# When the reciprocals of three blocks' denominators are taken in the keys stage of a decoder layer

## The chip, the cores and the metric

The kernel runs on one core of a Trainium2 chip. The metric is the device time of one execution in microseconds (us), the median of three runs; lower is better. Besides the times there is one execution recorded by the hardware profiler. A core has five engines that run side by side and wait for each other through semaphores: PE (matrix products; PEld is its weight loading), DVE (vector operations), ACT (activations and casts), POOL (a second, slower vector engine) and SP, which here only issues transfers (DMA). Each of them works through its own queue in order.

## The reference, cut to what matters

```python
x = x + attn(layernorm(x))             # linear attention, 16 heads, 128 features per head
x = x + xattn(layernorm(x), ctx)       # cross-attention to 154 context rows
x = x + ffn(layernorm(x))              # 8 experts, the 6 best per token, and a shared part

# attn, for each of 2 batches of 2048 tokens of width 512:
q_proj, k_proj = elu1(q @ proj), elu1(k @ proj)
kv    = einsum('bhnf,bhnd->bhfd', k_proj, v)
attn  = einsum('bhnf,bhfd->bhnd', q_proj, kv)          # numerators
z     = 1.0 / (einsum('bhnf,bhf->bhn', q_proj, k_proj.sum(axis=2)) + 1e-08)
out   = (attn * z[..., None]).reshape(b, n, d) @ w_out + b_out
```

Everything is in float32. The reciprocal `z` is what the change is about: one number for each token and head.

## The kernel before, in words

The 4096 tokens are 8 blocks of 512 (`nblk`), 4 to each batch (`bpb`). A product of full accuracy is written as three matrix multiplications of rounded parts (`product`, line 144).

The **keys stage** (lines 1323 to 1350) runs over the keys of all 8 blocks, 16 steps to a block, one for each chunk `c` of four heads and each tile `t` of 128 tokens. A step makes the key features (`key_features`: a matrix product `pp`, two ACT activations at lines 371 and 372, one DVE operation at line 373 and an addition on POOL at line 414) and now and then adds them to the sums (`key_values`, `pkv`). While the second batch's keys are worked, the same steps also make the query features of the first batch (`query_step`, `pqp`, from step 66 on), because that batch's sums are finished. When a chunk of queries is complete, `sums_step` takes its numerators (`pn`, copied by DVE at line 509 and stored by SP at line 510) and its denominators (`pd`). After the fourth chunk of a block, `reciprocals` is called.

Between the steps `dense` fills in other products: a list of generators that give one matrix multiplication at a time. Here these are the queries, keys and values of the next blocks (`pq`, `pk`, `pv`), and in the last block the keys and values of the context for the cross-attention (`xpk`, `xpv`). `dense` also is the clock of the program: `dense.after(n, do)` runs `do` when `n` more multiplications of the list have been recorded.

`reciprocals(b, pd)` (line 529) does in this order:

- DVE adds the small constant and copies `pd` out (`den`, line 532); SP writes it to memory in four pieces (`dd`, line 535).
- 10 products later (`turned`, line 541) SP loads it back as a tile `z` of 128 rows, so that the reciprocal is short.
- 26 products after the denominators (`stored`, lines 544 and 545) DVE takes the reciprocal of `z`, held at its place in the program's order, and SP stores the result (`zd`). The last block has 24.

The readers of `zd` are `load_reciprocals` (line 558, tiles `zr`, loaded by SP at the end of the keys stage and in the queries stage that follows) and then `attended` (line 570 on POOL, 571 on ACT, 118 on DVE). The attention's output products (`po_a`) follow, with the weight `wout`, which is loaded (`xswout`) and split into two parts (`split_weight`, lines 138 and 118: `wout_hi` on ACT, `wout_lo` on DVE and POOL) in the last block of the keys stage.

Three things tie the queues to each other. The banks of the accumulators are few: `pp` and `pqp` share four (`sc`), `pq`, `pn`, `pd`, `pkv`, `xpk` and the like share four others. The half tiles that hold `e_k`, `e_q`, `num`, `den` and `kf` share nine buffers (`kp`), so a new one may have to wait until SP has stored an old one. And each of SP's transfers waits for the one eight places before it.

The order in which the instructions stand in the queues is settled when the program is built: a scheduler with a modelled time line orders them within what the dependences allow (`schedule_with_timeline_sim=True`), except where `keep_in_program_order` holds one.

Of the kernel before, what the change touches and what calls it, by code (L numbers as in the profile page):

```python
# [37 lines left out]
def decoder_layer(  # L38
# [28 lines left out]
    nblk = tokens // TB  # L67
    bpb = nblk // batches
# [32 lines left out]
    def half(name, dtype=F32):  # L101
        return work.tile([P, 512], dtype, tag="kp", name=name, bufs=9)
# [115 lines left out]
    dense = Dense()  # L218
# [121 lines left out]
    for t in range(NT):  # L340
# [5 lines left out]
        b = nc.vector.tensor_tensor(lo, pt, hi.bitcast(F32), ALU.subtract)  # L346
# [167 lines left out]
    def denominators(b, c):  # L514
        if c == 0:
            pds[b] = bank(f"pd{b}")
        for h in range(4):
            columns.matmul(
                pds[b][h * HD : (h + 1) * HD, :],
                lhsT=kszs[b // bpb][:, c, h, :],  # L520
                rhs=qps.pop((b, c, h)),
                start=c == 0,
                stop=c == NC - 1,
                skip_group_check=True,
            )
        if c == NC - 1:
            reciprocals(b, pds.pop(b))

    def reciprocals(b, pd):

        den = half(f"den{b}")
        nc.vector.tensor_scalar(den, pd, Z_EPS, None, ALU.add)
        dd = dram.tile([4, NC, TB], F32, name=f"dd{b}")
        for h in range(4):
            nc.sync.dma_start(out=dd[h], in_=den[h * HD : h * HD + NC, :])
        z = small.tile([P, H * TB // P], F32, tag="z", name=f"z{b}", bufs=1)
        flat = "h c n -> (h c n)"
        zd = dram.tile([4, NC, TB], F32, name=f"zd{b}")

        def turned():  # L540
            nc.sync.dma_start(out=z, in_=dd.rearrange(flat).rearrange("(p n) -> p n", p=P))

        def stored():
            tc.keep_in_program_order(nc.vector.reciprocal(z, z))
            nc.sync.dma_start(out=zd.rearrange(flat).rearrange("(p n) -> p n", p=P), in_=z)

        dense.after(10, turned)
        dense.after(26 if b < nblk - 1 else 24, stored)
        zds[b] = zd

    def load_numerators(b):
# [771 lines left out]
    for n in range(nblk * per):  # L1323
        b, c, t = n // per, n // NT % NC, n % NT
# [38 lines left out]
    for n in range(len(steps) + 1):  # L1363
        if n < len(steps):
            b, c = steps[n]
# [41 lines left out]
    for n in range(len(steps) + LAG + 1):  # L1407
        if n < len(steps):
            b, c, t = steps[n]
# [46 lines left out]
        if n > LAG:  # L1456
            b, c, t = steps[n - LAG - 1]
# [187 lines left out]
```

## Time and profile before

| what | value |
|---|---|
| median of three runs | 2317.7 us (2314.31 to 2324.51) |
| the profiled execution | 2318.24 us, span 2316.5 us, mean PE clock 0.989 |
| PE, PEld busy | 2226.9 us (96%), 1729.3 us (75%) |
| DVE, ACT, POOL busy | 1682.5 us (73%), 1103.5 us (48%), 1231.5 us (53%) |
| transfers | 498.24 MB, mean 215 GB/s |
| reciprocals (line 544) | 8, the first three at 320.9, 380.8 and 453.4 us |
| DVE idle before those three, for the load of `z` | 0, 3.2 and 12.2 us |
| the three loads of `z` issued (line 541) | 319.0, 378.6 and 445.3 us |

A line of the profile names the source line, the engine, the operation and `output<-inputs`, with the number of instructions and their time. In a time line the first number is the start in us from the start of the span, the second the duration, and a bracket at the end gives the idle time of that engine just before and what ended it. In a table of waits the three numbers are the total in us, how many times, and the longest. In a table of windows each engine has its busy time in the stretch and its number of instructions, followed by the granted PE clock, the busy share of the 16 DMA engines and GB/s.

### The profile page before, as it was taken

To read this page: it belongs to the slowest core of one execution; us is meant where nothing else is said; L and a number is where in the kernel's file an instruction comes from. 1 tells how busy PE (TensorE), PEld (TensorE's weight loads), DVE (VectorE), ACT (ScalarE), POOL (GpSimd) and SP (SyncE) were. 2 spreads that over 40 slices of the span, in tenths; PEclk is the share of its full clock that TensorE was granted. 3 is DMA by queue.
4 is the path that set the end of the run, shared out by engine and by line. 5 is a ranking of instruction groups with operands and counts; after the bars stand their busy time and mean duration, and the time that the engine had idled before them with its cause. 6 is when DMAs were issued, how large, how long until landed. Compare 5 with 4: busy or idle time off the path is not lost.

```text
span 2316.5 us, 35269 instructions
## 1 busy us (share of the span) xinstructions
PE 2226.9 (96%) x11978; PEld 1729.3 (75%) x11978; DVE 1682.5 (73%) x2733; ACT 1103.5 (48%) x2598; POOL 1231.5 (53%) x1084
## 2 busy tenths in 40 slices
PE   7999999898989999989999999999999999999999
PEld 5888777555666777766787877888878888788887
DVE  6554565568586877768978767787797887877777
ACT  4555677656466777765343343222433223432221
POOL 5545433446475665544866454555484554755443
PEclk9999999999999999999999999999999999999999
DMA  6556777899975666566867647566557566575553
GB/s 212 177 172 178 204 220 213 231 261 274 245 226 147 188 191 172 155 183 215 298 237 258 223 182 294 224 225 239 188 190 274 225 235 236 194 282 205 209 191 132
DMA packets 199986, 498.24 MB, mean 215 GB/s; under 512 B 27450, under 2 KB 47290, under 8 KB 179870
## 3 DMA queue, kind: packets, MB, share of 16 engines
q1 hardware_dynamic: 196446, 483.60, 63.1%
q0 software_dynamic: 3360, 12.38, 1.8%
q8 instruction: 96, 1.57, 0.3%
q14 instruction: 84, 0.69, 0.1%
HBM read 351.30 MB, written 144.60 MB: 214 GB/s over the span
## 4 chain that ended last, share of the span: by engine, by line
PE 73%; DMA 12%; DVE 6%; issue 4%; POOL 3%; ACT 2%; SPq 1%; POOLq 0%; DVEq 0%; ACTq 0%
PE pg L1099 29%; PE pf L1212 11%; PE pf L148 4%; PE pk L148 3%; PE pv L148 3%; PE po_x L148 3%; PE pq L148 3%; PE xpq L148 3%; PE pp L409 2%; PE pc L752 2%; PE xpt L732 2%; PE psc L700 1%; PE pkv L230 1%; DMA x<-xr_x 1%; DMA qst<-qd 1%
## 5 line engine op out<-in xcount | busy, mean ns | idle before, releaser
L1099 PE MATMUL pg<-xo,wq 128*128 128x512 f32 x3360 | 821.9, 392 | 3.2 <-DVE u L1113 1.5
L1099 PEld LDWEIGHTS pg<-xo,wq 128*128 128x128 f32 x3360 | 628.6, 188 | 142.8 <-DVE u L1113 3.0
L414 POOL TENSOR_TENSOR kacc<-kacc,e_k 128x512 f32<-128x512 f32 x128 | 166.1, 1298 | 228.3 <-DVE e_k L373 205.5
L1233 DVE TENSOR_TENSOR sum<-sum,pf 128x512 f32<-128x512 f32 x376 | 252.3, 683 | 44.4 <-PE pf L1212 40.5
L710 ACT ACTIVATE xe<-psc,nb 128x154 f32<-128x154 f32 x512 | 196.2, 411 | 80.6 <-DVE nb L707 72.2
L715 POOL TENSOR_TENSOR xe<-xe,sm 128x616 f32<-128x616 f32 x128 | 155.6, 1226 | 79.8 <-DVE sm L714 70.4
L1212 PE MATMUL pf<-ht,wdo 128*128 128x512 f32 x696 | 185.7, 393 | 5.3 <-DVE sum L1233 5.3
L1162 POOL TENSOR_TENSOR u<-u,gr 128x512 f32<-128x512 f32 x48 | 63.6, 1325 | 210.7 <-DVE u L1131 210.0
L373 DVE SCALAR_TENSOR_TENSOR e_k<-pp,e_k 128x512 f32<-128x512 f32 x128 | 87.4, 685 | 107.0 <-ACT e_k L372 101.1
L1212 PEld LDWEIGHTS pf<-ht,wdo 128*128 128x128 f32 x696 | 130.1, 188 | 35.8 <-DVE sum L1233 7.1
L1130 ACT ACTIVATE u<-u 128x512 f32<-128x512 f32 x80 | 50.6, 633 | 206.5 <-DVE u L1119 206.5
L1212 PE MATMUL pf<-hb,wdo 128*128 128x512 f32 x522 | 146.7, 397 | 0.0
L148 PE MATMUL pf<-wd,hp 128*128 128x512 f32 x528 | 134.0, 401 | 5.2 <-DVE mv_n L248 3.4
L707 DVE TENSOR_REDUCE nb<-psc 128x2 f32<-128x308 f32 x256 | 112.4, 467 | 29.0 <-PE psc L700 28.6
L148 PEld LDWEIGHTS pf<-wd,hp 128*128 128x128 f32 x528 | 99.4, 190 | 34.1 <-issue 6.5
L1119 DVE TENSOR_TENSOR u<-u,pg 128x512 f32<-128x512 f32 x160 | 108.4, 681 | 11.1 <-PE pg L1099 9.9
L710 ACT ACTIVATION_READ_ACCUMULATOR xe<-psc,nb 128x1 f32 x512 | 115.4, 225 | 0.0
L1212 PEld LDWEIGHTS pf<-hb,wdo 128*128 128x128 f32 x522 | 97.2, 188 | 23.0 <-DVE sum L1233 1.7
L371 ACT ACTIVATE e_k<-pp 128x512 f32<-128x512 f32 x128 | 76.8, 601 | 70.9 <-PE pp L409 60.7
L700 PE MATMUL psc<-xkst,xst 96*128 96x154 f32 x512 | 91.7, 287 | 9.6 <-ACT xe L710 7.9
L700 PEld LDWEIGHTS psc<-xkst,xst 96*128 96x128 f32 x512 | 77.8, 195 | 23.1 <-ACT xe L710 14.5
L409 PEld LDWEIGHTS pp<-pst,kst 96*128 96x128 f32 x512 | 75.5, 190 | 24.7 <-issue 8.9
(290 smaller groups left out, 5131.5 us busy)
## 6 DMA issues: line engine op xcount, KB each, us to landing
wq<-wqs SPq DMA_DIRECT2D x90, 1024.0 KB
wqs<-wq SPq DMA_DIRECT2D x30, 1024.0 KB
wdo<-wds SPq DMA_DIRECT2D x29, 1024.0 KB
kst<-kd SPq DMA_DIRECT2D x96, 256.0 KB
qst<-qd SPq DMA_DIRECT2D x96, 256.0 KB
xst<-xqd SPq DMA_DIRECT2D x96, 256.0 KB
wdo<-wds SPq DMA_DIRECT2D x29, 768.0 KB
kd<-khl SPq DMA_DIRECT2D x32, 512.0 KB
```

The source lines that it names most:

```text
L148: nc.tensor.matmul(dst, lhsT=a, rhs=b, start=n == 0, stop=n == len(todo) - 1)
L373: nc.vector.scalar_tensor_tensor(e, src, 0.0, e, ALU.max, ALU.add)
L409: nc.tensor.matmul(pp[:, h], lhsT=stks[b, c][:, h, rows], rhs=pst[:, head], start=True, stop=True)
L414: nc.gpsimd.tensor_tensor(acc, acc, kp, ALU.add)
L700: nc.tensor.matmul(psc[:, i], lhsT=xsts[b, c][:, h, t * P : (t + 1) * P], rhs=ksts[bt, c][:, h, :], start=True, stop=True,)
L707: nc.vector.tensor_reduce(nb[:, two], psc, AX.X, ALU.max, negate=True)
L710: nc.scalar.activation(e[:, h, :], psc[:, i], AF.Exp, bias=nb[:, h : h + 1], accum_out=sm[:, h : h + 1],)
L715: nc.gpsimd.tensor_tensor(e, e, sm.unsqueeze(2).to_broadcast([P, 4, keys]), ALU.mult)
L1099: nc.tensor.matmul(pb, lhsT=w[:, p, i, k, :], rhs=xop[:, q, k, :], start=first and m == 0, stop=m == len(todo) - 1, skip_group_check=True,)
L1119: nc.vector.tensor_tensor(dst, dst, pb, ALU.add)
L1212: nc.tensor.matmul(banks[i], lhsT=w[:, p, i * P : (i + 1) * P], rhs=t[q], start=new and m == 0, stop=m == len(TERMS) - 1, skip_group_check ...
L1233: nc.vector.tensor_tensor(dst, dst, banks[i], ALU.add)
```

## The change

For blocks 0, 1 and 2 (`b < bpb - 1`) the reciprocal and its store are recorded 60 products after the denominators; for all others they stay where they were. The load of `z` stays 10 products behind.

```diff
         dense.after(10, turned)
-        dense.after(26 if b < nblk - 1 else 24, stored)
+        dense.after(60 if b < bpb - 1 else 26 if b < nblk - 1 else 24, stored)
         zds[b] = zd
```

In the built program the number of operations on each engine is the same. What stands elsewhere:

- DVE: in blocks 0, 1 and 2 the reciprocal moves back by 18, 14 and 14 instructions. In block 2 it stood between the split of the context's value weight (`xwv_lo`) and `eq_1_1`; now it stands behind `xkhl` of the first context key.
- SP: the three stores of `zd` move back by 9, 12 and 18 transfers. In block 2 the store stood between the loads of the third and the fourth row of `wout`; now it stands behind the first store of a context key (`ckd`). In blocks 0 and 1 it now stands just ahead of the next block's key loads (`kst_0`).
- PE and ACT: up to the cross-attention the order is that of before, but for one group of four key products that is no longer split.
- The opening of the cross-attention (its first two blocks, from the second chunk of heads on) is ordered differently on every engine: the score products (`psc`) stand up to three halves of a tile later between the others. On POOL the four products with `zr` of block 7 (line 570) stand together ahead of the softmax product `xe_1_1`, and some row additions (line 319) stand one to two softmax products (line 715) earlier. After that the orders agree again to the end.

## The prediction

> **What bounds the kernel now.** I read the head of the page first, then the waits between 300 and 545 us, where the three moved reciprocals lie, then the engines' time lines around the longest wait, and last the windows, for the transfers.
>
> ```profile
> span 2316.5 us, 35269 instructions
> PE 2226.9 (96%) x11978; PEld 1729.3 (75%) x11978; DVE 1682.5 (73%) x2733; ACT 1103.5 (48%) x2598; POOL 1231.5 (53%) x1084
> ```
>
> PE is busy in 96% of the span, so 89.6 us is all that it idles; a change that takes no work from PE can only shorten those.
>
> ```profile
> DVE z L544 <- DMA z<-dd: 15.4, 2, 12.2
> PE pqp L486 <- DVE eq L373: 11.0, 3, 9.9
> ACT wout_hi L138 <- DMA xswout<-in_w_out: 7.0, 2, 5.8
> ```
>
> DVE waits twice for a load of z before a moved reciprocal, 3.2 us (block 1) and 12.2 us (block 2); block 0 waits nothing. Only the long one has an answer on PE, 9.9 us. The third line is a wait in ACT's queue in the same microseconds, and it will matter.
>
> ```profile
> 453.38 0.55 DVE L544 RECIPROCAL z<-z 128x64 f32<-128x64 f32 x1 [12.21 <-DMA z<-dd]
> 453.85 0.63 DVE L373 SCALAR_TENSOR_TENSOR eq<-pqp,eq 128x512 f32<-128x512 f32 x1
> 454.53 0.80 PE L486 MATMUL pqp<-qst,pst 96*128 96x512 f32 x1 [9.94 <-DVE eq L373]
> 455.26 1.08 PE L230 MATMUL pkv<-e_k,va 128*32 128x128 f32 x16
> ```
>
> The reciprocal stands at the head of DVE's queue from 441.2 us. Behind it stands eq_1_1, whose read frees the bank that PE's next query product needs; so PE stops at 444.6 and starts at 454.5.
>
> ```profile
> 445.33 0.34 SPq L541 DMA_DIRECT2D z<-dd x1
> 453.96 0.33 SPq L545 DMA_DIRECT2D zd<-z x1
> 444.70 0.60 ACT L371 ACTIVATE e_k<-pp 128x512 f32<-128x512 f32 x1 [4.05 <-DMA dd<-den]
> 455.59 1.27 ACT L138 CAST wout_hi<-xswout 128x512 fp32r<-128x512 f32 x2 [5.77 <-DMA xswout<-in_w_out]
> ```
>
> The load of z is issued at 445.3 and has landed by 453.4: 8.05 us for 32 KB. SP stands still for 5.7 us of that with the store of zd (its last issue before ends at 448.25). ACT waits on a load of wout until 455.59, later than z lands.
>
> ```profile
> 350.00:400.00 50.00, 50.00 (x374) 35.05 (x373) 27.98 (x44) 35.10 (x67) 17.43 (x14) 1.00 0.77 222
> 440.00:450.00 10.00, 4.59 (x34) 3.45 (x22) 1.17 (x1) 5.77 (x12) 4.35 (x4) 0.87 0.99 282
> 450.00:460.00 10.00, 5.47 (x42) 2.84 (x43) 6.01 (x10) 2.98 (x6) 3.66 (x3) 0.62 0.89 278
> 460.00:490.00 30.00, 27.43 (x218) 18.23 (x217) 24.29 (x39) 19.72 (x39) 15.93 (x13) 1.00 1.03 293
> ```
>
> Columns: stretch, length, busy PE, PEld, DVE, ACT, POOL, then PE clock, DMA share and GB/s. PE lost nothing around block 1's wait. Around block 2's the DMA engines were full, and stayed full to 490.
>
> **The change, part by part.** No instruction is added or removed, so all is in the waits.
>
> *Blocks 0 and 1.* DVE gets back 0 and 3.2 us, but PE was busy for 49.8 and 50.0 of the 50 us around: worth 0. The stores of zd move to about 8 us later; their first reader is issued at 463.4, some 75 us after the second. The stores now stand ahead of the next block's key loads in SP's queue and wait for a reciprocal that follows khl_0 and eq_2_1 on DVE (0.68 and 0.55 us). Those key loads have to wait for the landing of kd anyway (6.21 us in the chain at 426 us), and that hides it; without that cover it would be 2 to 3 us for each of two blocks.
>
> *Block 2, the most there is to win.* PE's idle 9.94 us. Then PE ran slowly: the same work (one pqp, 16 pkv, 8 pn, 8 pd) took 4.18 us from 454.53 to 458.71 and 2.71 us from 467.50 to 470.21, so 1.47 us more; the window's clock of 0.62 is the same thing. Together 11.4 us.
>
> *What is late next.* ACT's order is unchanged, and before 449.8 it waits for nothing that DVE owed it. So: eq_1_1's activation ends at 445.81, DVE frees the bank at 446.5, and PE starts its query product at 446.5, 8.0 us earlier. It has 2.7 us of pqp, pkv, pn, pd and then two context products of 12 (0.14 us each), and is through them at about 453.5. The third context product needs a bank that DVE empties with kf_0, and kf_0 stands behind the split of wout's third row, which needs ACT's cast, which needs the load that ACT started on at 455.59. Nothing ahead of that load changes in SP's queue. Casts end at 456.9, the split (0.75) at 457.6, kf_0 (0.54) at 458.2: PE waits about 4.7 us. The query product after it (pqp_2_1) needs eq_1_3, whose activation stands behind four casts: 457.4, then three first activations at 0.5 and one second at 0.63, DVE 0.68: PE at 460.3 against 465.03 before, 4.7 us won. Two query products on, behind ACT's queue, it is 464.0 against 467.50: 3.5 us.
>
> *The transfers.* SP no longer stands still for 5.7 us, but the engines were 0.99 and 0.89 busy in those 20 us: only 0.1 + 1.1 = 1.2 us was free, so what SP's queue brings (the zr and xr_a loads that POOL waits for near 490) comes 1.2 us earlier, not 3.5. The gain out of this stage lies between 1.2 and 3.5. I take 3.5, because no wait of PE between 460 and 550 names a transfer; the lower end stays in the range.
>
> *The reciprocal at its new place* follows the first xkhl, near 462 us; z landed by 453.4, so it waits for nothing and costs its 0.55 us on a DVE that idles. Its store waits with it behind one ckd store; the readers are issued near 481.
>
> Two rules of the Trainium skill stand against these rows. "DMA: Bandwidth & Descriptors", section "Anatomy of one DMA", gives about 2 us plus bytes over 436 GB/s: by it z would take an estimated 2.1 us, land at 447.4, and the wait that the change removes would be 6 us shorter, half the prize; the measured 8.05 us decides. The same page ("Issuing engines are not separate DMA queues") says that transfers of all issuers interleave on the same engines, which would make every microsecond given back on SP worthless while they are full: by it alone the gain is the 1.2 us above.
>
> *The opening of the cross-attention* is reordered, which the reciprocals do not ask for; its cost must be taken from the stalls that are there.
>
> ```profile
> 722.80 1.26 POOL L319 TENSOR_TENSOR xr_x<-xr_x,bor 128x512 f32<-128x512 f32 x1 [5.08 <-DMA xr_x<-x]
> 725.29 0.46 PE L733 MATMUL tail<-ident,xe 128*104 128x128 f32 x1 [4.04 <-POOL xe L715]
> POOL xr_x L319 <- DMA xr_x<-x: 18.0, 5, 5.9
> POOL xr_a L319 <- DMA xr_a<-in_x: 7.6, 2, 6.0
> ```
>
> POOL waits for a row's load, with softmax products queued behind, and PE waits 0.96 and 4.04 us for them. In the new order these row additions stand one product earlier, so one more softmax product (1.22 us) comes after the wait: I take +1.2 us. Ends: 5.0 us won if the waits no longer reach PE, 5.5 lost if the two longest (5.47 and 5.08) reach it whole.
>
> *Sum.* 3.5 − 1.2 = 2.3 us won. On the profiled execution's own 2318.24 us that is 2315.9; it lies 0.5 us over the median of 2317.7, and on the median it is **2315.4 us**. Its own range: 3.5 + 5.0 = 8.5 won to 5.5 − 1.2 = 4.3 lost, 2309.2 to 2322.0.
>
> **The rivals.** *The whole stall comes back.* If wout's loads land earlier once SP's queue runs freely, ACT's wait shrinks with DVE's and PE keeps 11.4 us: 2306.3, and down to 2301.3 with the 5.0 us of the opening. For it: wout's second and third rows are issued at 446.7 to 448.3, only 1.3 us after z. Against it: they are issued before the stall of SP, not behind it, and ACT's 5.77 us is measured beyond z's landing.
>
> *Nothing comes through.* The full DMA engines give back 1.2 us, and the opening takes 1.2: 2317.7. For it the shares of 0.99 to 1.03; against it that PE's waits after 460 are on DVE and ACT.
>
> *Slower: POOL's queue in the cross-attention.* PE needs the softmax product xe_2_3 at the end of a chunk; before, its scores were made at 682.1 and POOL delivered it at 689.4, 7.3 us. Counting PE's work in the new order between the two places gives 8.2 us, so 0.9 us is the slack. If a row addition that now stands ahead waits longer than this, the waits of POOL (18.0 + 7.6 us) go to PE instead of the 5.0 it pays now, and PE restarts slowly once (1.5): 22.1 us lost, less 3.5, so 2336.3. For it: POOL is over 70% busy there. Against it: before, most of POOL's waits cost PE nothing.
>
> That the change does not do what it says is excluded: the built order shows the reciprocal moved.
>
> **How the numbers follow.** The forecast 0.45, nothing 0.10, the whole stall 0.27, POOL's queue 0.18. A measurement of this kernel tells about 0.5% from no change, that is 2306.1 to 2329.3. The whole-stall case straddles its edge: 0.23 faster, 0.04 same. POOL's queue likewise: 0.15 slower, 0.03 same. So faster 0.23, same 0.62, slower 0.15. The range reaches over most of the whole-stall case and the lower part of POOL's: 2303 to 2328.
>
> **What would show it.** Right: no DVE wait for z before 460 us; PE's gap of 9.94 replaced by one of about 5 that ends after the cast of wout; pqp_2_1 near 460; the same PE order from the third cross block on. Wrong: no gap after 446 us (whole stall), or PE waits on softmax products of over 10 us between 655 and 770.

## The result, and the profile after

The changed kernel takes 2323.9 us (median of 12 runs, 2319.85 to 2331.67) against 2317.38 us of before (12 runs, 2313.31 to 2324.51). The ratio is 1.0025, with a 95% interval of 1.0014 to 1.0035: 5.8 us slower (6.5 us by the medians), where 2.3 us faster was forecast. It lies inside the predicted range of 2303 to 2328 us, but its sign is the other one. Measured again beside other kernels it was 1.0033 (1.0020 to 1.0045).

The profiled execution happens to be among the fastest of its kernel: 2320.64 us, 2.4 us over that of before.

```profile
span 2318.9 us, 35269 instructions
PE 2229.3 (96%) x11978; PEld 1732.3 (75%) x11978; DVE 1682.2 (73%) x2733; ACT 1103.4 (48%) x2598; POOL 1230.3 (53%) x1084
```

The waits of after between 300 and 545 us (total, times, longest):

```profile
ACT wout_hi L138 <- DMA xswout<-in_w_out: 7.6, 3, 3.7
DVE wout_lo L118 <- ACT wout_hi L138: 6.2, 1, 6.2
PE xpk L148 <- DVE kf L617: 5.4, 1, 5.4
PE pqp L486 <- DVE eq L373: 0.8, 1, 0.8
```

DVE no longer waits for z before 462 us, and PE's stop of 9.94 us on eq is gone. In its place stands the wait that the prediction named: ACT on the load of wout, DVE on ACT's cast, PE on kf. The time lines of DVE and PE there:

```profile
456.88 0.69 DVE L118 TENSOR_TENSOR wout_lo<-xswout,wout_hi 128x512 fp32r<-128x512 f32 x1 [6.19 <-ACT wout_hi L138]
457.49 0.53 DVE L617 TENSOR_SCALAR kf<-xpk,bk_sb 128x308 f32<-128x308 f32 x1
458.08 0.62 PE L148 MATMUL xpk<-ct,xwk_hi 128*128 128x308 f32 x1 [5.38 <-DVE kf L617]
461.32 0.63 PE L486 MATMUL pqp<-qst,pst 96*128 96x512 f32 x1
465.77 1.08 PE L230 MATMUL pkv<-e_k,va 128*32 128x128 f32 x16
469.19 1.07 PE L230 MATMUL pd<-eq,ksz 128*32 128x512 f32 x3
470.90 0.44 PE L486 MATMUL pqp<-qst,pst 96*128 96x512 f32 x1
```

The query product pqp_2_1 starts at 461.32, 3.7 us earlier than before. But PE is then slow: 16 pkv take 1.08 us (0.65 in before at 467.92), a group of pd 1.07 (0.61), and only the product at 470.90 is at full speed again. The same product started at 470.71 in before. As after had been 0.54 us late at 425 us, the whole stage won 0.35 us. The windows say the same (busy PE, PEld, DVE, ACT, POOL, then PE clock, DMA share, GB/s):

```profile
440.00:450.00 10.00, 9.94 (x88) 6.91 (x87) 6.67 (x10) 6.32 (x13) 7.31 (x6) 1.00 0.96 291
450.00:460.00 10.00, 4.62 (x27) 4.38 (x27) 1.94 (x4) 3.98 (x8) 2.68 (x3) 0.85 1.02 312
460.00:490.00 30.00, 28.33 (x189) 17.05 (x189) 22.65 (x38) 18.64 (x36) 13.66 (x11) 0.82 0.99 281
```

From 460 to 490 PE is busier than before (28.33 us, 27.43 before), at a clock of 0.82 where it was 1.00. That goes towards explaining a missing gain; it does not explain a loss. So two theories were tested: *order*, in which the reordered opening of the cross-attention costs the 6 us, and *keys stage*, in which the reciprocals and their transfers cost it.

### The profile page after: what moved, and what is told of

It is laid out like the page before. It is cut to its first block, busy times and chain, and to the rows that moved or that the text cites. A ratio compares the mean times of both kernels' runs of the same rounds, so it can differ in the third digit from the quotient of the medians.

```text
span 2318.9 us, 35269 instructions
## 1 busy us (share of the span) xinstructions
PE 2229.3 (96%) x11978; PEld 1732.3 (75%) x11978; DVE 1682.2 (73%) x2733; ACT 1103.4 (48%) x2598; POOL 1230.3 (53%) x1084
## 4 chain that ended last, share of the span: by engine, by line
PE 71%; DMA 11%; DVE 7%; issue 4%; POOL 3%; ACT 2%; SPq 1%; POOLq 0%; DVEq 0%; ACTq 0%
PE pg L1099 28%; PE pf L1212 11%; PE pk L148 4%; PE pv L148 3%; PE pq L148 3%; PE pf L148 3%; PE po_x L148 3%; PE xpq L148 3%; PE pp L409 2%; PE pc L752 2%; PE pkv L230 2%; PE xpt L732 1%; DMA x<-xr_a 1%; PE psc L700 1%; DMA x<-xr_x 1%
## 5 line engine op out<-in xcount | busy, mean ns | idle before, releaser
L715 POOL TENSOR_TENSOR xe<-xe,sm 128x616 f32<-128x616 f32 x128 | 155.6, 1226 | 72.8 <-DVE sm L714 60.8
```

The source lines that it names most:

```text
L715: nc.gpsimd.tensor_tensor(e, e, sm.unsqueeze(2).to_broadcast([P, 4, keys]), ALU.mult)
```

## The experiments

Every ratio is to the kernel before, timed beside the changed one; in brackets stands its 95% interval.

### Which part of the change costs

**Block 2 alone, block 0 alone.**

```diff
-        dense.after(60 if b < bpb - 1 else 26 if b < nblk - 1 else 24, stored)
+        dense.after(60 if b == 2 else 26 if b < nblk - 1 else 24, stored)   # block2_alone
+        dense.after(60 if b == 0 else 26 if b < nblk - 1 else 24, stored)   # block0_alone
```

> Only block 2's reciprocal is 60 products behind; blocks 0 and 1 stay at 26, and every engine's order after the keys stage is that of before. Theory 'two places': what block 2 wins at its 9.94 us gap is given back by the wait for wout and by the half clock after it, so the PE stands at the same product at 471 us as before (within 0.6 us), and the time is that of before: 2316.5 to 2317.5, ratio 0.9995 to 1.0003. Rival 'keys stage': the lost 6 us arise here (transfers of block 2, or the slow clock), ratio 1.0015 or more. The prediction on record made it 3.5 us won: 0.9985.

> Only block 0's reciprocal is 60 products behind. That alone gives the cross-attention the order that the whole change gives it; block 2 keeps its stall of 9.9 us at 454 us. Theory 'two places': the new order of the cross-attention's opening costs the 5 to 6 us, so 2322 to 2323.5, ratio 1.002 to 1.0026, with the PE waits on softmax products up between 650 and 750 us. Rival 'keys stage': the order is worth what the prediction gave it, 1.2 us lost, ratio 1.0005 or less.

Block 2 alone: 1.0003 (0.9988 to 1.0018). Block 0 alone: 1.0017 (1.0004 to 1.0031). The part that was to bring the gain brings nothing (the 3.5 us forecast would be 0.9985, outside the interval), and the part that the prediction held worthless costs.

**Two thirds of the change, the change again, and block 0 by four products.**

```diff
+        dense.after(60 if b in (1, 2) else 26 if b < nblk - 1 else 24, stored)   # blocks_1_and_2
+        dense.after(30 if b == 0 else 26 if b < nblk - 1 else 24, stored)        # block0_at_30
```

> Blocks 1 and 2 at 60, block 0 at 26: two thirds of the change, with the orders of PE, ACT and POOL all as before. Theory 'order': nothing of the loss, ratio 0.9990 to 1.0005 (the 1 to 2 us that block 2 gave back in the trace of block 2 alone, at most). Rival 'keys stage': most of the loss, ratio 1.002.

> The changed kernel once more, beside the other three, for a second trace of it. Both theories: ratio 1.002 to 1.003 (about 2322 to 2324). In the trace, theory 'order': between 640 and 770 us it falls 3 to 5 us behind the kernel before, and block 2 gives at most 2 us back between 440 and 500 us. If the keys stage were the cause, the 3 to 5 us would be lost by 640 us.

> Block 0's reciprocal four products later than before (30 instead of 26), six places on in DVE's queue; blocks 1 and 2 at 26. Nothing else moves in the keys stage, but the cross-attention gets the order of the changed kernel. Theory 'order': the loss is there in full, ratio 1.0015 to 1.0025, with 3 to 5 us lost between 640 and 770 us. Rival (the long delay of block 0 itself costs, through the stores and loads in SP's queue): ratio 1.0000 to 1.0005.

Blocks 1 and 2: 1.0000 (0.9988 to 1.0012). The whole change: 1.0033 (1.0020 to 1.0045). Block 0 at 30: 1.0023 (1.0008 to 1.0037). A reciprocal moved by six places in DVE's queue costs about as much as the whole change. In the built program the order at 28 products is that of before in every queue; at 30 PE, ACT and POOL have the order of the changed kernel throughout. So the loss belongs to the order, not to the late reciprocals.

The traces place it. I take the time from the seventh reciprocal of z (line 544, near 618 us) to the 257th activation of the softmax (line 710, near 860 us), each start read from the time line:

| order of the opening | kernels | us |
|---|---|---|
| as before | before, before_again, block2_alone, blocks_1_and_2, numerators_late_block2 | 239.9, 242.4, 239.6, 239.0, 239.5; mean 240.1 |
| changed | after, whole_change_again, block0_alone, block0_at_30 | 241.5, 244.9, 245.2, 248.4; mean 245.0 |

That is 4.9 us of the 5.8 to 7.7. Each entry is one execution, and block0_at_30's is the slowest of its twelve (2335.07 us); without it the difference is 3.8 us. The first pair of traces, 239.9 and 241.5, was the mildest, which is why comparing those two alone showed little. The remaining 1 to 4 us are within what single traces scatter and are not placed.

### Where in the opening

PE's waits on the softmax products of POOL between 640 and 780 us, in before, in the changed kernel's second trace (whole_change_again) and in block0_at_30:

```profile
PE tail L733 <- POOL xe L715: 5.0, 2, 4.0
```

```profile
PE tail L733 <- POOL xe L715: 6.7, 4, 4.7
```

```profile
PE tail L733 <- POOL xe L715: 8.6, 6, 3.4
```

In the five traces of the table with the old order this wait is 3.5 to 5.0 us in total, in the four with the changed one 5.8 to 8.6: some 3 of the 4.9 us.

POOL's time line around 690 us, first of before, then of whole_change_again, there with SP's issue of the row's load:

```profile
677.42 5.66 POOL L715 TENSOR_TENSOR xe<-xe,sm 128x616 f32<-128x616 f32 x4
683.02 0.85 POOL L289 DMA_DIRECT2D x<-x  x1
683.90 2.54 POOL L118 TENSOR_TENSOR xwo_lo<-xsxwo,xwo_hi 128x512 fp32r<-128x512 f32 x2
688.21 1.22 POOL L715 TENSOR_TENSOR xe<-xe,sm 128x616 f32<-128x616 f32 x1 [1.77 <-DVE sm L714]
690.09 1.22 POOL L715 TENSOR_TENSOR xe<-xe,sm 128x616 f32<-128x616 f32 x1 [0.67 <-DVE sm L714]
691.27 2.55 POOL L319 TENSOR_TENSOR xr_a<-xr_a,bout 128x512 f32<-128x512 f32 x2
```

```profile
686.21 0.85 POOL L289 DMA_DIRECT2D x<-x  x1
686.95 0.33 SPq L318 DMA_DIRECT2D xr_a<-in_x  x1
692.73 1.27 POOL L319 TENSOR_TENSOR xr_a<-xr_a,bout 128x512 f32<-128x512 f32 x1 [5.67 <-DMA xr_a<-in_x]
693.97 2.54 POOL L118 TENSOR_TENSOR xwo_lo<-xsxwo,xwo_hi 128x512 fp32r<-128x512 f32 x2
696.47 2.37 POOL L715 TENSOR_TENSOR xe<-xe,sm 128x616 f32<-128x616 f32 x2
```

Before, the row addition of tile a7_1 stood behind the softmax products xe_2_2, xe_2_3 and xe_3_0, and its load had landed by then (the additions at 691.27). In the changed order it stands right behind the issue of the next block's load, ahead of the two splits of xwo and of those three products. POOL reaches it at 687.06, 0.1 us after SP has issued the row's load, and waits 5.67 us with all of that behind it. In block0_alone the same wait is 6.17 us, in block0_at_30 6.71 (where the profile puts its end down to another load, of xst), and in the mild trace of after 1.67. In the five traces with the old order it is 0 in three, 2.25 in before_again and 2.85 in numerators_late_block2.

That place is further ahead than the list under "The change" has it: not one to two, but three softmax products and two splits earlier, which at 1.22 us and 2.54 us for the two splits is an estimated 6.2 us of POOL's work.

**The row additions on another engine.** Eight additions of the attention's last two blocks go to DVE, in the kernel before and in the changed one.

```diff
-        nc.gpsimd.tensor_tensor(xs, xs, row, ALU.add)
+        (nc.vector if name[:2] in ("a6", "a7") else nc.gpsimd).tensor_tensor(xs, xs, row, ALU.add)
```

> All reciprocals as before (26). In the cross-attention's opening the eight row additions of the attention's last two blocks (xr_a) run on DVE instead of POOL, so no softmax product stands behind a row's load on POOL. The schedule of that stage is a third one. Theory 'POOL's queue': PE's waits on POOL's softmax products there fall below the 4 to 5 us of before, and 0 to 4 us are won, ratio 0.998 to 1.000. Rival: DVE, which is about three quarters busy there, becomes the wait, 1 to 3 us lost.

> The whole change (blocks 0, 1 and 2 at 60) with the same eight row additions on DVE. From the cross-attention on, every engine's order is now the same as in the kernel with only the row additions on DVE; the keys stage differs by the three reciprocals alone. Theory 'order': with the order made equal the change costs nothing, the two kernels lie within 0.0007 of each other. Rival 'the late reciprocals themselves': it is slower than the other by 0.002 to 0.003, as the whole change was.

0.9999 (0.9988 to 1.0011) and 1.0006 (0.9993 to 1.0019). PE's wait of tail on POOL's xe is gone from both traces, and the stretch of the table takes 238.3 and 237.5 us. Against before, the change no longer costs anything that is told from zero. Between these two kernels it costs 0.0007 by the ratios, the edge of what was expected, and 3.0 us by the medians (2318.81 and 2321.77), so this pair alone leaves room for a small cost of the late reciprocals; blocks_1_and_2 (1.0000) shows none. The 1.8 to 2.6 us won in the stretch against the mean of before did not show in the time.

**The one load left out.**

```diff
+        if name == "a7_1":
+            nc.gpsimd.tensor_tensor(xs, row, row, ALU.add)
+        else:
             nc.sync.dma_start(out=xs, in_=src)
             nc.gpsimd.tensor_tensor(xs, xs, row, ALU.add)
```

> The whole change, with one row's load left out: for the second tile of the attention's last block (a7_1) the 128 rows of x are not loaded and not added, and POOL adds the bias row to itself instead (256 KB less to load, that part of the residual left out). In the changed order this addition stands on POOL ahead of two softmax products, and in the four traces with that order POOL waited 1.7, 5.7, 6.2 and 6.7 us there for the load. Everything else keeps the changed order but for a few neighbours that change places. Theory 'that one wait is the cost of the order': most of the loss goes, ratio 0.9995 to 1.0010, and POOL waits under 1 us before that addition. Rival 'the order costs elsewhere' (the softmax products in another sequence, PE waits on DVE and ACT): ratio stays at 1.0020 to 1.0033.

0.9999 (0.9989 to 1.0009). POOL's time line of this kernel:

```profile
684.67 1.19 POOL L319 TENSOR_TENSOR xr_a<-bout 128x512 f32<-128x512 f32 x1 [1.11 <-DMA x<-xr_a]
686.68 2.57 POOL L118 TENSOR_TENSOR xwo_lo<-xsxwo,xwo_hi 128x512 fp32r<-128x512 f32 x2
689.18 2.40 POOL L718 TENSOR_TENSOR xe<-xe,sm 128x616 f32<-128x616 f32 x2
```

(Its code is three lines longer, so L718 is the L715 of the others.) With POOL's wait at 1.1 us, and that for a store, the xe pair starts at 689.18 instead of 696.47, the stretch takes 236.7 us (in the fastest of its twelve executions), and the loss of the whole change is gone, although the three reciprocals are still late. Every queue also has neighbours that changed places between 680 and 735 us (6 places on POOL, 12 on PE), and 256 KB less are loaded. Their share is not separated from that of the wait: what is shown is that the loss lies in the order around this one row, and the wait is the part of it that the traces show.

### Where the expected gain went

**The kernel before, a second trace.**

> The kernel before once more, for a second trace. Theory: PE's stop for z, 9.9 us in the trace that the prediction read, is 4 to 5 us here, as in the three other traces that have the reciprocal at its old place (5.0, 4.1 and 3.9 us), because z's load takes about 4 us and not 8; the prize was one large sample. Rival: the 9.9 us are typical of this kernel (over 8 us again), and the others are short because of what was changed in them.

```profile
445.99 0.34 SPq L541 DMA_DIRECT2D z<-dd  x1
449.59 0.55 DVE L544 RECIPROCAL z<-z 128x64 f32<-128x64 f32 x1 [6.20 <-DMA z<-dd]
450.74 0.79 PE L486 MATMUL pqp<-qst,pst 96*128 96x512 f32 x1 [3.93 <-DVE eq L373]
```

The load of z takes 3.60 us here from issue to reciprocal, and PE stops for 3.93 us. Of six traces with the reciprocal at its old place, five have stops of 3.4 to 5.0 us (rows_on_dve 3.40, split_late 3.88, before_again 3.93, block0_at_30 4.05, block0_alone 5.04). The 9.94 us that the prediction read were the exception. With the reciprocal at 60 the stop for kf is 4.3 to 5.7 us in all six traces that have wout's casts at their old place and its loads undisturbed (whole_change_again 4.31, rows_on_dve_whole 4.40, block2_alone 4.59, blocks_1_and_2 5.06, after 5.38, one_row_not_loaded 5.7). One stop of about 4 us is exchanged for one of about 5.

The same exchange shows in the time that PE takes between two query products (line 486), those that start at 426.74 and 470.71 us in before. It is 44.0 us in before and 39.0 to 44.3 in the five traces with block 2 at 26 (before, before_again, block0_alone, block0_at_30, rows_on_dve), mean 42.0. In the six with it at 60 (those just listed for kf) it is 41.1 to 43.6, mean 42.4. Nothing is won on the mean, and a single trace lies up to 3 us off it.

**Wout's casts held back**, without and with block 2 at 60.

```diff
-                nc.scalar.copy(hi[:, k], part)
+                cast = nc.scalar.copy(hi[:, k], part)
+                if keep:                      # True for wout alone
+                    tc.keep_in_program_order(cast)
```

> All reciprocals at 26, as before; the four casts of wout are held at their place in the program, behind the last query features of the keys stage, so ACT and DVE no longer wait there for its load. The wait for z stays. Both theories: the gap of 9.9 us ahead of 454 us stays, as the reciprocal stands where it stood, and the time is that of before within 3 us (2314 to 2320); the casts, now in one heap near 500 us, may cost 1 to 2 us there.

> The kernel with wout's casts held back, and block 2's reciprocal 60 products behind. Against the one with the casts held back alone only the reciprocal and its store stand elsewhere. Theory 'wout is next': with that wait out of the way there is no gap over 2 us between 445 and 470 us, no half clock, and 9 to 12 us are won against the kernel with the casts held back alone (about 2306). Rival 'transfers are next': the DMA engines are full, another load holds the PE, and 1 to 4 us are won.

1.0036 (1.0024 to 1.0048) and 1.0030 (1.0018 to 1.0042). The first is a miss: 1 to 2 us were expected. PE waits 4.20 us at 497.7 for a query feature and 3.75 at 590 for a row. But holding the casts gave every queue another order, in places up to some 1050 us, as its trace shows, so the loss cannot be put down to the heap of casts alone. The two kernels share that order but for a few places near 460 us, and their difference can be read: block 2's late reciprocal wins 1.8 us by the medians (2328.3 to 2326.48), less than either kernel scatters (8.5 and 11.8 us), and not 9 to 12. With it PE indeed runs through 440 to 460 us without a stop (9.96 and 10.00 us busy in the two halves, clock 1.00). Then it stops elsewhere; the waits of split_late_block2 from 455 to 500 us:

```profile
ACT e_k L373 <- DMA numd<-num: 4.2, 1, 4.2
DVE xkhl L118 <- DMA zr<-zd: 4.0, 1, 4.0
PE pkv L232 <- DVE e_k L375: 3.3, 1, 3.3
```

ACT waits for a store to empty a half tile, DVE's split of a context key for the cast that stands behind this on ACT (it ends at 471.74 us, the split starts at 471.77; the table puts the wait down to a load of zr), and PE for a key feature that stands behind the split on DVE. The DMA share is 0.93 and 1.02 in the two halves of 440 to 460 us.

**The numerators' load moved.** The 1 MB load of the first numerators goes from step (7, 3, 0) to (7, 3, 2) and is held there, with block 2 at 60.

```diff
+        if (b, c, t) == (nblk - 1, 3, 2):
+            load_numerators(0)        # its dma_start now under tc.keep_in_program_order
```

> Block 2 at 60, blocks 0 and 1 at 26, and the 1 MB load of the first numerators held on POOL behind the key sums of step 3,1, some 20 us later than at 445 us; with it the casts and splits of wout move a few places back. Theory 'transfers set the pace from 440 to 500 us': the waits for wout shrink and no gap over 3 us stands before 465, but the same megabyte is moved later and its readers wait near 490 to 500 us; 0 to 3 us are won, ratio 0.9985 to 1.0000. Rival 'single waits': with z and wout out of the way the whole stall and the slow clock go, 9 to 12 us won, ratio 0.995 to 0.996.

1.0005 (0.9994 to 1.0017). No gap of PE between 440 and 500 us is over 2.5 us any more, and the time has not moved: there are now five of 1.2 to 2.5 us. This rules out the large gain of single waits. It came out a little above the 0.9985 to 1.0000 of the other theory, with which its interval overlaps. No version tried beats the kernel before.

## Why the prediction was wrong

*Blocks 0 and 1 worth nothing.* Right for their waits and stores: with block 1 late as well as block 2 the ratio is 1.0000, and block 0 costs no more at 60 products than at 30 (1.0017 and 1.0023).

*The most there is to win, 11.4 us.* Wrong in size. It was read from one trace, in which z took 8.05 us; in five others PE's stop is 3.4 to 5.0 us.

The rule of the Trainium skill that was set against it ("DMA: Bandwidth & Descriptors", section "Anatomy of one DMA", an estimated 2.1 us) was nearer to the 3.5 to 3.9 us of those five than the row was. The measurements decide here too: the load takes 1.4 to 1.8 us longer than the rule, which that page gives for the path of POOL while this transfer is SP's.

*What is late next.* Right: the same tile, the same chain, 5.4 us against 4.7, and pqp_2_1 3.7 us earlier against 4.7.

*3.5 us carried out of the stage.* This step failed. The prediction charged the slow clock to the stop that goes (1.47 us) and nothing to the stop that comes. In after PE worked from 458.1 to about 470.7 at half speed, and of 3.7 us 0.35 was left. In most other traces the clock came back sooner, but there the stop that goes is only 3.4 to 5.0 us and one of 4.3 to 5.7 takes its place: 42.0 us for the stretch at the old place, 42.4 at the new. The term measured about nothing: 1.0003 for block 2 alone.

*The opening, 1.2 us lost.* This step gave the result its sign: the term measured 4.9 us (3.8 without the slowest trace), near the 5.5 of its lower end. It was sized by one softmax product that comes to stand behind a wait of unchanged length. But three products and two splits stand behind it, and the wait itself became longer, 1.7 to 6.7 us instead of 0 to 2.9, because the addition moved ahead of the time at which its row lands. That the length of a wait depends on when the queue reaches it was the thing left out. With about 0 won and 4.9 lost the sum comes to 4.9 of the 5.8 us measured; the rest is not placed.

*The rival of POOL's queue* had this mechanism, and even its condition: 0.9 us of slack for a row addition that waits longer. Its price was wrong in the other direction. It took all of POOL's waits over to PE (22.1 us), where one wait of 1.7 to 6.7 us moved. *The whole stall comes back* is excluded by blocks_1_and_2, and *nothing comes through* was right for the keys stage. Whether for its reason, the full DMA engines, is not settled: the stop at z gave way to other waits each time, but no run here has these stages with the engines less full.

## What to carry to other kernels

A prize read from a single stall of a single trace is a sample: bound it with other stretches or a second trace, and charge a slow clock to the stall that follows, not only to the one that goes. When a scheduler reorders a stage that the change does not touch, look in each in-order queue for an instruction that waits for a load, and ask whether it now stands ahead of the landing, and what stands behind it. Here six places of one reciprocal near 320 us put one row addition near 690 us ahead of its row, and that cost more than the change could win.

## What the runs showed of the hardware that was not expected

The half clock after a stop had no fixed length. In before, PE was slow for 3.2 us of work after a stop of 9.94 us (454.5 to 457.7). In after it was slow for some 12.6 us after one of 5.38 us. In whole_change_again, after 4.31 us, it ran slow to 463.0, at full speed to 466.7 and slow again to 469.5; the mean clock of 445 to 480 us was 0.90 there and 0.80 in after, with the same work in the same order. The Trainium skill ("TensorE: Matmul & The Clock Gate", section "Part 1: The HAM clock gate") gives about 3.4 us of sustained work for the return of the full clock. Before agrees with its 3.2 us; after, whose PE shows no gap from 458.1 on and was slow for 12.6 us, does not. In all fourteen traces here each stretch of half clock between 440 and 480 us lasted one to four times 3.41 us: 3.41 or 6.83 in most, 10.24 in before, 13.65 in after and in rows_on_dve_whole. What decides how many was not tried.

The same 32 KB load of z took 3.46 to 3.92 us in five traces and 8.05 in one, with the DMA engines about full in all six (a share of 0.93 to 1.02 from 445 to 480 us, 0.99 with the slow one). What made the one slow stays open.
